# Layer 0 of a four-layer convolution net: the patch filter and the 3x3 taps folded into one map per channel

## The chip, the cores and the metric

The kernel runs on one core of one Trainium2 chip. A core has five engines with queues of their own: TensorE (PE in the profile; its weight loads are PEld), VectorE (DVE), ScalarE (ACT), GpSimd (POOL) and SyncE (SP), which here issues loads. 16 DMA engines move data between HBM and the on-chip memory SBUF; matrix products land in PSUM, which has 8 banks of 512 fp32 columns on 128 partitions. The metric is the device time of one execution in microseconds (us). All data is fp32.

## The reference

The input is x, 4 images of 64 channels of 256x256. Four layers follow each other, each of the form `x = x + layer(group_norm(x))`. Only layer 0 changes:

```python
def _gn(v, G=32, eps=1e-5):               # 32 groups of 2 channels, over the whole image
    ...
def _L0_conv_ref(x, w_in, w_dw, fft_filter, w_out):
    p = 8
    x = einsum('bchw,oc->bohw', x, w_in)             # 64 -> 384 channels
    xp = x.reshape(B, C, H//p, p, W//p, p).transpose(0, 1, 2, 4, 3, 5)
    xf = rfft2(xp) * fft_filter                      # one 8x5 filter per channel
    x = irfft2(xf) ... back to (B, C, H, W)          # within each 8x8 patch
    x = conv_general_dilated(x, w_dw, 3x3, padding 1, feature_group_count=C)
    x1, x2 = split(x, 2, axis=1)                     # 192 gates, 192 values
    x = gelu(x1) * x2
    return einsum('bchw,oc->bohw', x, w_out)         # 192 -> 64 channels
x = x + _L0_conv_ref(_gn(x), ...)
x = x + _L1_conv_ref(_gn(x), kernel)                 # dense 3x3, 64 -> 64
x = x + _L2_conv_ref(_gn(x), ...)                    # two 1x1 branches chosen by a mask
x = x + _L3_conv_ref(_gn(x), ...)                    # 2D FFT with 2 x 16x16 modes
```

The patch filter is linear and works inside an 8x8 patch; the 3x3 taps are linear too and reach one pixel into the neighbouring patches. Both act on each of the 384 channels alone.

## The kernel before

Layer 0 goes over 128 strips of 8 rows (32 for each image). For a strip it normalizes x on ACT (`normalize_x`, L256), transposes it on PE so that pixels lie on partitions (`transpose_x`, L396), takes each 8x8 patch to 64 real frequencies with a matrix (`transform_x`, L406), expands 64 to 384 channels (`expand`, L419) and multiplies by the filter while DVE moves the result out of PSUM (L422), and goes back to pixels with a matrix that also puts channels on partitions (`invert`, L457, moved out by ACT at L464). The 3x3 taps follow in two ways: for 256 of the 384 channels on PE, as nine products with 32x32 diagonal matrices (`depthwise`, L484: 16 of these side by side in the array), for the last 128 on DVE as eight multiply-adds over 2048 elements (`vector_tap`, L522). Then come GELU on ACT (L498, L530), the gate on DVE (L504, L537), the product with w_out (`project`, L550 and L559), the residual (L573), the sums for the next normalization (L581), and the store to x1 by POOL's queue (L590). Intermediate results stay in SBUF.

The order on PE, DVE, ACT and SP is written out by hand (`tc.manual_schedule`): the loop over t interleaves stages of strips t-1 to t+2. POOL's order is left to the tile framework. PSUM is four tiles of two banks, taken in turn by `pair`. Loads of x and of the residual are tied to chosen matmuls by `after`, so that they come spread over the strip. Sums for images 1 to 3 are taken on the way (`load_stats`, `next_stats`); those for image 0 come first of all.

Of the kernel before, what the change touches and what calls it, by code (L numbers as in the profile page):

```python
# [26 lines left out]
def _patch_dft():  # L27


    p = PATCH  # L30
    h, w = np.meshgrid(np.arange(p), np.arange(p), indexing="ij")
    rows, pick = [], []
    for kw in range(p // 2 + 1):
        edge = kw in (0, p // 2)
        for kh in range(p // 2 + 1 if edge else p):
            ang = 2 * np.pi * (kh * h + kw * w) / p
            sel = np.zeros((p, p // 2 + 1))
            sel[kh, kw] += 0.5 if edge else 1.0
            if edge:
                sel[(-kh) % p, kw] += 0.5  # L40
            rows.append(np.cos(ang).ravel())
            pick.append(sel.ravel())
            if not (edge and kh in (0, p // 2)):
                rows.append(np.sin(ang).ravel())
                pick.append(sel.ravel())
    fwd = np.array(rows)
    inv = np.linalg.inv(fwd)
    pick = np.array(pick)
    twice = lambda m: np.concatenate([m, m], 0)
    return twice(fwd.T), twice(inv.T), twice(pick).T  # L50
# [19 lines left out]
def _constants(H, W):  # L70
    f_blk, b_blk, pick = _patch_dft()
# [17 lines left out]
        "c_ident": np.eye(128), "c_avg32": avg32, "c_sel32": sel32, "c_fdft": f_blk, "c_bdft": b_blk, "c_pick": pick, "c_avg": avg, "c_avgp": avgp, "c_avgx": avgx,  # L89
# [5 lines left out]
def _layouts(i):  # L95


    order = np.r_[0:128, HID : HID + 128, 128:HID, HID + 128 : 2 * HID]
# [3 lines left out]
        "w_in": a["L0_conv_w_in"][order].T,  # L102
        "w_dw": a["L0_conv_w_dw"].reshape(2 * HID, 9)[order].reshape(3, 128, 9).transpose(1, 0, 2),
        "filt": a["L0_conv_fft_filter"].reshape(2 * HID, 40)[order].T,
        "w_out": a["L0_conv_w_out"].T,
# [13 lines left out]
class _Net:  # L119
    def __init__(self, ctx, tc, a):  # L120
# [15 lines left out]
        self.slots = ctx.enter_context(tc.tile_pool(name="slot", bufs=2))  # L136
# [138 lines left out]
    def _layer0(self, ctx, dst):  # L275
# [5 lines left out]
        def pair(name):  # L281

            return pp.tile([128, 2, 512], F32, tag=f"p{next(turn) % 4}", name=name)

        small = self.small = lambda name: pair(name)[:, 0, :]
        HW2 = W // 2
        NJ = H // 8
        NS = B * NJ
        Q = 32
        halves = [slice(0, C), slice(C, 128)]  # L290
        quarters = [slice(k * Q, (k + 1) * Q) for k in range(4)]

# [9 lines left out]
        with tc.tile_pool(name="l0a", bufs=1) as p_a:  # L302
            bst0 = new_bst0(0)

            flat = a["x"][0].rearrange("c (s h) w -> (c s) (h w)", s=2)
            avgs = [self.load(name, p_a) for name in ("c_avgp", "c_avgx")]
            for k in range(NJ):
                if k % 2 == 0:
                    two = self.slot(k // 2 % 3, f"st_{k}").rearrange("p r w -> p (r w)")
                t = two[:, 4 * W * (k % 2) : 4 * W * (k % 2 + 1)]  # L310
                nc.sync.dma_start(t, flat[:, 4 * W * k : 4 * W * (k + 1)])
                input_stats(t.rearrange("p (r w) -> p r w", w=W), k, bst0)
            self.group_norm(0, 0, bst0, avgs)

        cp = pool("l0c", 1)
        p_st, p_x, p_r, p_xn = pool("l0st", 2), pool("l0x", 2), pool("l0r", 2), pool("l0xn", 1)
        p_T, p_f, p_u, p_l = pool("l0xT", 1), pool("l0xf", 2), pool("l0up", 2), pool("l0l", 1)
        p_v, p_g, p_h = pool("l0v", 2), pool("l0g", 1), pool("l0h", 2)
        fdft, bdft = self.load("c_fdft", cp), self.load("c_bdft", cp)
        pick, filt = self.load("c_pick", cp), self.load("filt", cp)  # L320
        wdw = self.load("w_dw", cp)
        ps = small("psf")
        nc.tensor.matmul(ps[:, :384], pick, filt, start=True, stop=True)
        flt = cp.tile([128, 1, 384], F32, name="flt")
        nc.vector.tensor_copy(flt[:, 0, :], ps[:, :384])

        win = cp.tile([128, 384], F32, name="win")
        for s in range(2):
            nc.sync.dma_start(win[halves[s]], a["w_in"])

        wout = cp.tile([128, 4, C], F32, name="wout")
        for k in range(4):
            nc.sync.dma_start(wout[quarters[k]], a["w_out"][0:128].rearrange("(g q) o -> q g o", q=Q))
        woutc = cp.tile([128, C], F32, name="woutc")
        for s in range(2):
            nc.sync.dma_start(woutc[halves[s]], a["w_out"][128:HID])

        eye = cp.tile([128, Q], F32, name="eye")
        nc.vector.tensor_copy(eye, self.ident[:, 0:Q])
        for k in range(1, 4):  # L340
            nc.vector.tensor_add(eye, eye, self.ident[:, k * Q : (k + 1) * Q])
        diag = cp.tile([128, 2, 9, Q], F32, name="diag")
        for t in range(2):
            for k in range(9):
                nc.vector.tensor_scalar(diag[:, t, k, :], eye, wdw[:, t, k : k + 1], None, ALU.mult)

        place = lambda t: divmod(t, NJ)
        exists = lambda t: 0 <= t < NS
        x0, xns, xT, xf, ups, yt, lt, vt, ht, rt, po, bst1, gt = ({} for _ in range(13))

        def load_x(t, *sides, ins=None):
            b, j = place(t)
            if t not in x0:
                x0[t] = p_x.tile([128, 8, HW2], F32, tag="x", name=f"x0_{t}")
            for s in sides:
                d = nc.sync.dma_start(
                    x0[t][halves[s]], a["x"][b, :, 8 * j : 8 * j + 8, s * HW2 : (s + 1) * HW2]
                )
                if ins:
                    self.after(d, ins)  # L360


        def rows_of(t):
            b, j = place(t)
            if j > 0:
                return [(b, 8 * j - 2, 0, 4)]
            parts = [(b - 1, H - 2, 0, 1)] if t > 0 else []
            return parts + ([(b, 0, 1, 4)] if t < NS else [])

        def load_r(t, *sides, ins=None):  # L370
            if t not in rt:
                rt[t] = p_r.tile([128, 4, 2, HW2], F32, tag="r", name=f"r0_{t}")
            for b, row, lo, hi in rows_of(t):
                for s in sides:
                    d = nc.sync.dma_start(
                        rt[t][halves[s], lo:hi].rearrange("p k r w -> p (k r) w"),
                        a["x"][b, :, row : row + 2 * (hi - lo), s * HW2 : (s + 1) * HW2],
                    )
                    if ins:
                        self.after(d, ins)  # L380

        def normalize_x(t):
            if not exists(t):
                return

            xn = xns[t] = p_xn.tile([128, HW2 // 16, 2, 8, 8], F32, tag="xn", name=f"xn_{t}")
            self.normalize(
                xn.rearrange("p k n r w -> p r (k n) w"),
                x0.pop(t).rearrange("p r (m w) -> p r m w", w=8), 0, place(t)[0],
            )  # L390

        def transpose_x(t):
            xn = xns.pop(t)
            ps = pair(f"psT_{t}").rearrange("p z (k m) -> p (z k) m", m=128)
            for k in range(8):
                nc.tensor.transpose(ps[:, k, :], xn[:, k].rearrange("p n r w -> p (n r w)"), self.ident)  # L396
            xT[t] = p_T.tile([128, 8, 128], F32, tag="xT", name=f"xT_{t}")
            nc.scalar.copy(xT[t], ps)

        def transform_x(t):  # L400
            x = xT.pop(t)
            ps = pair(f"psF_{t}").rearrange("p n (k m) -> p n k m", m=C)
            for k in range(8):
                for n in range(2):
                    for s in range(2):
                        nc.tensor.matmul(  # L406
                            ps[halves[s], n, k], x[halves[n], k, halves[s]], fdft[halves[n]], start=True, stop=True
                        )
            xf[t] = p_f.tile([128, 2, 8, C], F32, tag="xf", name=f"xf_{t}")
            nc.scalar.copy(xf[t], ps)  # L410

        def expand(t, g, k):

            if k == 0:
                ups[t, g] = p_u.tile([128, 2, 4, 384], F32, tag="up", name=f"up_{t}_{g}")
            ps = pair(f"psu_{t}_{g}_{k}")
            for s in range(2):
                for n in range(2):
                    nc.tensor.matmul(  # L419
                        ps[halves[n], s, 0:384], xf[t][halves[s], n, 4 * g + k], win[halves[s]], start=True, stop=True  # L420
                    )
# [163 lines left out]
        def store(t, *sides, ins=None):  # L585
            if t not in rt:
                return
# [149 lines left out]

# [724 lines left out]
```

## Time and profile before

The kernel takes 7382.61 us (median of 3 runs, 7378.16 to 7394.91). The profiled execution has a span of 7394.8 us from its first instruction to its last; the page gives no other time for it, and the span is 12.2 us above the median.

| stretch (from the trace) | us | PE busy | DVE busy | ACT busy | DMA share | GB/s |
|---|---|---|---|---|---|---|
| start, sums of image 0 (0 to 90) | 90 | 27.22 | 57.66 | 14.21 | 0.61 | 216 |
| strips of layer 0 (90 to 4852) | 4762 | 4688.79 | 4384.48 | 2330.40 | 0.24 | 58 |
| layer 1 (4852 to 5532) | 680 | 669.71 | 607.83 | 486.54 | 0.91 | 220 |
| layer 2 (5532 to 6822) | 1290 | 1255.00 | 1117.73 | 1003.75 | 0.67 | 171 |
| layer 3 (6822 to 7395) | 573 | 507.53 | 268.79 | 93.66 | 0.93 | 358 |

The first matmul of layer 1 starts at 4851.89 us. In a group of instructions the profile gives the time in which at least one of them ran, and the mean of one: 16 small matmuls that run side by side count once in the first number. The DMA share is the mean busy share of the 16 DMA engines[...].

### The profile page before, as it was taken

The numbers are of one execution on the slowest core, as the hardware profiler recorded it, in microseconds if no ns is written. First come the engines' busy times: TensorE is split into PE (matmuls) and PEld (weight loads), VectorE is DVE, ScalarE is ACT, GpSimd is POOL, SyncE is SP. The second block draws the span as 40 slices with busy tenths as digits, with TensorE's granted clock in tenths as the row PEclk, the third lists the DMA queues.
The fourth block names the chain that finished last, engine by engine and source line by source line (L and its number), as shares of the span: only waits on it lengthen the run. The fifth ranks groups of instructions, "written<-read, shape, count | busy, mean of one in ns | idle before, by whom it ended". The sixth has DMA issues, their size and how long they took to land. (4 is left out here: it accounts for less than half of the span.)

```text
span 7394.8 us, 396673 instructions
## 1 busy us (share of the span) xinstructions
PE 7148.3 (97%) x188280; PEld 4274.7 (58%) x188280; DVE 6436.5 (87%) x5625; ACT 3928.6 (53%) x4181; POOL 659.3 (9%) x1435
## 2 busy tenths in 40 slices
PE   6999999999999999999999999999999999999998
PEld 4666666666666666666666666633334444444376
DVE  7999999999999999999999999889988888897445
ACT  3444444454454444444445545457778778776211
POOL 0000000000000000000000000011111222222011
PEclk9999999999999999999999999999999999999955
DMA  3222222222222222222111111279986676676989
GB/s 131 64 64 64 61 64 61 61 61 61 61 61 61 61 61 61 61 61 61 47 46 47 47 47 47 60 186 228 230 197 158 169 178 173 172 179 192 354 328 400
DMA packets 650136, 873.38 MB, mean 118 GB/s; under 512 B 43988, under 2 KB 470180, under 8 KB 646468
## 3 DMA queue, kind: packets, MB, share of 16 engines
q1 hardware_dynamic: 567492, 579.51, 29.4%
q0 software_dynamic: 81024, 268.50, 12.5%
q8 instruction: 1477, 24.20, 1.4%
q14 instruction: 143, 1.17, 0.1%
HBM read 579.41 MB, written 268.44 MB: 115 GB/s over the span
## 5 line engine op out<-in xcount | busy, mean ns | idle before, releaser
L484 PE MATMUL psd<-y,diag 32*32 32x512 f32 x73296 | 2535.6, 597 | 12.4 <-issue 10.7
L522 DVE SCALAR_TENSOR_TENSOR v<-y,sb_w_dw,v 128x2048 f32<-128x2048 f32 x1024 | 2391.5, 2335 | 112.1 <-ACT v L520 89.3
L484 PEld LDWEIGHTS psd<-y,diag 32*32 32x32 f32 x73296 | 1526.9, 103 | 858.8 <-issue 338.9
L464 ACT COPY y<-psy 128x512 f32<-128x512 f32 x1536 | 915.6, 660 | 1673.5 <-PE psy L457 1671.7
L422 DVE TENSOR_TENSOR up<-psu,flt 128x768 f32<-128x768 f32 x1024 | 933.1, 952 | 203.9 <-PE psu L419 203.2
L457 PEld LDWEIGHTS psy<-sb_c_bdft,up 64*64 64x64 f32 x49152 | 850.2, 135 | 343.3 <-issue 129.8
L457 PE MATMUL psy<-sb_c_bdft,up 64*64 64x64 f32 x49152 | 919.5, 221 | 25.0 <-issue 22.4
L419 PE MATMUL psu<-win,xf 64*64 64x384 f32 x8192 | 785.0, 488 | 20.9 <-DVE h L504 10.4
L1040 DVE TENSOR_TENSOR q<-xn 128x2313 f32<-128x2313 f32 (+2 forms) x256 | 627.8, 2494 | 1.7 <-ACT xn L256 1.7
L1095 PE MATMUL one<-z,wp 32*32 32x512 f32 x16384 | 594.1, 598 | 17.3 <-issue 13.4
L1041 ACT ACTIVATE q<-q 128x2313 f32<-128x2313 f32 (+2 forms) x256 | 528.9, 2086 | 31.4 <-DVE q L1040 29.9
L498 ACT ACTIVATE h<-psd 128x1024 f32<-128x1024 f32 x258 | 251.2, 1023 | 519.8 <-PE psd L484 519.7
L256 ACT ACTIVATE xn<-x,nb,r 128x1024 f32<-128x1024 f32 (+3 forms) x272 | 486.9, 1793 | 22.2 <-DMA x<-x 8.3
L1095 PEld LDWEIGHTS one<-z,wp 32*32 32x32 f32 x16384 | 368.4, 103 | 225.0 <-issue 82.7
L1054 PE MATMUL div<-q,ones 64*32 64x512 f32 x8192 | 466.2, 594 | 14.3 <-ACT q L1041 9.4
L429 POOL MEMSET y<- 128x22 f32 x384 | 52.2, 136 | 4264.3 <-ACT y L437 3209.8
L419 PEld LDWEIGHTS psu<-win,xf 64*64 64x64 f32 x8192 | 299.5, 134 | 192.1 <-issue 87.7
L1128 POOL DMA_DIRECT2D x<-r x512 | 273.6, 541 | 972.1 <-DVE r L1125 881.2
L854 PE MATMUL m<-t,wk 64*64 64x512 f32 x3072 | 341.1, 588 | 0.0
L1054 PEld LDWEIGHTS div<-q,ones 64*32 64x32 f32 x8192 | 151.8, 107 | 321.1 <-issue 253.6
L537 DVE TENSOR_TENSOR v<-g,v 64x1024 f32<-64x1024 f32 x257 | 313.2, 1219 | 9.3 <-ACT g L530 1.4
L504 DVE TENSOR_TENSOR h<-h,psd 128x1024 f32<-128x1024 f32 x258 | 302.7, 1215 | 7.5 <-PE psd L484 7.0
(156 smaller groups left out, 7400.4 us busy)
## 6 DMA issues: line engine op xcount, KB each, us to landing
x<-x SPq DMA_DIRECT2D x240, 640.0 KB, 6.3
x<-x SPq DMA_DIRECT2D x100, 1024.0 KB, 13.9
x<-in_x_dram SPq DMA_DIRECT2D x256, 256.0 KB, 3.8
x<-o POOLq DMA_DIRECT2D x128, 512.0 KB, 8.1
r<-x SPq DMA_DIRECT2D x512, 128.0 KB, 4.0
x<-r POOLq DMA_DIRECT2D x512, 128.0 KB, 4.0
r<-in_x_dram SPq DMA_DIRECT2D x248, 256.0 KB, 3.8
x<-r POOLq DMA_DIRECT2D x248, 256.0 KB, 3.3
```

The lines of the kernel that those rows point to most:

```text
L256: self.nc.scalar.activation(dst, src, AF.Identity, bias=self.nb[n][p0:p1, b : b + 1], scale=self.r[n][p0:p1, b : b + 1])
L419: nc.tensor.matmul(ps[halves[n], s, 0:384], xf[t][halves[s], n, 4 * g + k], win[halves[s]], start=True, stop=True)
L422: nc.vector.tensor_mul(ups[t, g][:, :, k, :], ps[:, :, 0:384], flt.broadcast_to([128, 2, 384]))
L457: nc.tensor.matmul(ps[halves[c], n, s, :, k, :], up[halves[n], s, k, i * 128 + c * C : i * 128 + (c + 1) * C], bdft[halves[n]], start=True ...
L464: nc.scalar.copy(yt[t][i][:, 3:11, w0 : w0 + 64].rearrange("p r (k n w) -> p n r k w", k=4, n=2), ps[:, :, s])
L484: ins = nc.tensor.matmul(d[q // 2][quarters[j], q % 2], diag[quarters[q], i, k, :], rows_in(t, i, quarters[q], j, dy)[:, :, dx : dx + W], ...
L522: nc.vector.scalar_tensor_tensor(v, s, wdw[:, 2, k : k + 1], v, ALU.mult, ALU.add)
L854: nc.tensor.matmul(rows2(m)[halves[j], s], w[dx][halves[s]], ts[n][halves[s], i, 2 * j : 2 * j + 2, dx : dx + W], start=(dx == 0), stop=(d ...
L1040: nc.vector.tensor_sub(d, p0, p1)
L1041: nc.scalar.activation(d, d, AF.Square)
L1054: ins = nc.tensor.matmul(ps[quarters[j], h], ones[halves[h]], q[n, g, k][halves[h], r + 2 * j : r + 2 * j + 2, o : o + W], start=(m == 0), ...
L1095: ins = nc.tensor.matmul(rows2(ps[g])[quarters[j], k], w[quarters[i]], z[quarters[i], h, 2 * j + dy : 2 * j + dy + 2, dx : dx + W], tile_p ...
```

## The change

The frequency route goes. The filter and the taps together are a linear map from a channel's patches to its output pixels, and that map depends on the channel alone. If the output cell is an 8x8 patch shifted by one pixel down and right, it needs 64 inputs of its "own" patch, and few of the right, lower and lower right neighbours. `tables` and `weights` build these maps on the chip at the start (128 channels at a time, copies on ACT and POOL) and write them to DRAM as `wts`.

The main loop works on 12 blocks (3 for each image), each of 11 cell rows: 11 x 34 = 374 columns. The 384 channels are taken in four parts of 96 (`kb`). For each part:

- `expand`: for each of 11 or 12 patch rows, 32 matmuls with the pixels as the stationary side and 96 columns of w_in as the moving side, so that pixels land on partitions; three copies (ACT and DVE by turns) put them into the one tile `u`, channel-major.
- `convolve`, 12 times: two gate and two value channels at once: 8 matmuls for the own patch (64x64, 374 columns) and 24 for the neighbours (16, 28 and 4 output rows); GELU on ACT, the gate on DVE, and a store of the result `h` to DRAM (`gs`) by POOL's queue. Its weights are loaded by `load_w`, one load for two convolves, three loads ahead.
- After `expand` and after the seventh convolve comes one `unit()`: the projection of one of 8 pixel rows of the block before. `load_g` reads its `g` back from DRAM with channels on partitions, `load_r` the residual; 32 matmuls, two adds, three sums, and a store.

PSUM becomes two tiles of four banks (`quad`). x for the next block is loaded and normalized between the convolves of the last part. After block 12 eight units remain by themselves. Layers 1 to 3 stay as they are; their SBUF slots are now taken after layer 0.

```diff
-        def pair(name):
-            return pp.tile([128, 2, 512], F32, tag=f"p{next(turn) % 4}", name=name)
+        def quad(name):
+            return pp.tile([128, 4, 512], F32, tag=f"p{next(turn) % 2}", name=name)
+        p_xn, p_x, p_st = pool("l0xn", NR + 1), pool("l0x", 2), pool("l0st", 2)
+        p_w, p_h = pool("l0w", 4), pool("l0h", 3)
...
+        def load_x(row, p_x=p_x):
+            b, i = row
+            x0[row] = p_x.tile([128, P, HW2], F32, tag="x", name=f"x0_{b}_{i}")
+            for s in range(2):
+                nc.sync.dma_start(x0[row][halves[s]], a["x"][b, :, P * i : P * i + P, s * HW2 : (s + 1) * HW2])
...
+        def expand(p, kb, t):
+            b, i0 = blocks[p]
+            ps = quad(f"psu_{p}_{kb}_{t}")
+            xn = xns[b, i0 + t]
+            for k in range(2):
+                for m in range(4):
+                    for s in range(2):
+                        for odd in range(2):
+                            nc.tensor.matmul(
+                                ps[halves[1 - odd], 2 * s + k, 2 * PB * m : 2 * PB * (m + 1)],
+                                xn[halves[s], 2 * (4 * k + m) + odd].rearrange("p r w -> p (r w)"),
+                                win[halves[s], kb, PB * (1 - odd) : PB * (3 - odd)], start=True, stop=True,
+                            )
...
+            nc.scalar.copy(at(slice(0, 128), 1), first)
+            lo, hi = halves
+            (nc.vector.tensor_copy if t % 2 else nc.scalar.copy)(at(hi, E2 + 1), second[lo])
+            nc.vector.tensor_copy(at(lo, O1), second[hi])
...
+        def convolve(p, kb, g):
+            ps = quad(f"pc_{p}_{kb}_{g}")
+            G = NG * kb + g
+            w = wl[p * (HID // 8) + G // 2]
...
+            for k in range(2):
+                for c in range(2):
+                    for h in range(2):
+                        nc.tensor.matmul(
+                            out(C * c, C, k, h), w[halves[h], k, 2 * (G % 2) + c, 0:C], cells(h, 4 * g + 2 * k + c, 0, 0),
+                            start=True, stop=False, tile_position=(h * C, c * C), skip_group_check=True,
+                        )
+            for n, (c0, m, down, right) in enumerate(UNITS):
...
+            nc.scalar.activation(h, v[:, 0], AF.Gelu)
+            nc.vector.tensor_mul(h, h, v[:, 1])
...
+            nc.gpsimd.dma_start(gs[p][:, 2 * G : 2 * G + 2].rearrange("k c p l -> (c p) k l"), h)
...
+        def load_g(p, r, half):
...
+                        nc.sync.dma_start(g1[halves[k], lo - q0 : hi - q0], gs[p][k, 0:C, at + lo : at + hi])
...
+        def load_unit(p, r):
...
+            load_r(p, r)
+            for half in range(2):
+                load_g(p, r, half)
...
+                for kb in range(4):
+                    for t in range(NR + 1):
+                        if 0 <= i0 + t < NP:
+                            expand(p, kb, t)
+                    unit()
+                    for g in range(NG):
+                        G = NG * kb + g
+                        if g % 2 == 0:
+                            load_w(p * (HID // 8) + G // 2 + 3)
+                        if kb == 3 and g < 2 and g < len(fresh):
+                            load_x(fresh[g])
+                        convolve(p, kb, g)
+                        self.next_norms()
+                        if g == NG // 2:
+                            unit()
+                        if kb < 3:
...
+                        else:
+                            for k in loaded[:1]:
+                                next_stats(b + 1, loaded.pop(0))
+                            if 0 <= g - 1 < len(fresh):
+                                k = g - 1
+                                normalize_x(fresh[k])
+                                if k + 2 < len(fresh):
+                                    load_x(fresh[k + 2])
```

The slices used above: `P` is 8, `PB` 48, `NG` 12, `NR` 11, `C` 64, `HID` 192; one packet of `h` in DRAM is a row of 374 fp32, 1496 bytes; one of the weights `w` is 1792 bytes; rows of x, residual and result are pieces of 128 fp32, 512 bytes.

## The prediction

> **What bounds the kernel now.** I read the slices first, then the stretches, then the groups of layer 0.
>
> Slices of the whole span (40 of 185 us):
>
> ```profile
> PE   6999999999999999999999999999999999999998
> PEclk9999999999999999999999999999999999999955
> DMA  3222222222222222222111111279986676676989
> ```
>
> PE is full from the second slice on; DMA idles for 26 slices, all of layer 0. The clock falls only at the end, in layer 3.
>
> Busy time by stretch (PE, PEld, DVE, ACT, POOL, then clock, DMA share, GB/s):
>
> ```profile
> 90.00:4852.00 4762.00, 4688.79 (x150103) 3091.40 (x150104) 4384.48 (x3604) 2330.40 (x2939) 245.66 (x679) 1.00 0.24 58
> 6822.00:7395.00 573.00, 507.53 (x3464) 334.12 (x3464) 268.79 (x474) 93.66 (x156) 53.52 (x74) 0.68 0.93 358
> ```
>
> In layer 0 PE (98%) ends nearly every wait and DVE (92%) is close behind; DMA has three quarters of its time free. The chain of waits reaches back only through layers 1 to 3, so here the stretch decides. Costliest groups:
>
> ```profile
> L484 PE MATMUL psd<-y,diag 32*32 32x512 f32 x73296 | 2535.6, 597 | 12.4 <-issue 10.7
> L522 DVE SCALAR_TENSOR_TENSOR v<-y,sb_w_dw,v 128x2048 f32<-128x2048 f32 x1024 | 2391.5, 2335 | 112.1 <-ACT v L520 89.3
> L464 ACT COPY y<-psy 128x512 f32<-128x512 f32 x1536 | 915.6, 660 | 1673.5 <-PE psy L457 1671.7
> L422 DVE TENSOR_TENSOR up<-psu,flt 128x768 f32<-128x768 f32 x1024 | 933.1, 952 | 203.9 <-PE psu L419 203.2
> L457 PE MATMUL psy<-sb_c_bdft,up 64*64 64x64 f32 x49152 | 919.5, 221 | 25.0 <-issue 22.4
> L498 ACT ACTIVATE h<-psd 128x1024 f32<-128x1024 f32 x258 | 251.2, 1023 | 519.8 <-PE psd L484 519.7
> L504 DVE TENSOR_TENSOR h<-h,psd 128x1024 f32<-128x1024 f32 x258 | 302.7, 1215 | 7.5 <-PE psd L484 7.0
> L854 PE MATMUL m<-t,wk 64*64 64x512 f32 x3072 | 341.1, 588 | 0.0
> L1054 PE MATMUL div<-q,ones 64*32 64x512 f32 x8192 | 466.2, 594 | 14.3 <-ACT q L1041 9.4
> ```
>
> The first number, divided by rounds of tiles that run together, is a round's price: m, four 64x64 tiles: 341.1/768 = 444 ns for 512 columns, 0.87 ns each; div, eight 64x32 tiles: 455 ns, 0.89; psy 75 ns for 64, 1.17; psd, 16 tiles: 553 ns.
>
> DMA prices, from stretches with one kind of packet (4 KB loads; 512-byte stores; 512-byte loads):
>
> ```profile
> 8.00:10.00 2.00, 0.00 (x0) 0.00 (x0) 1.99 (x5) 0.00 (x0) 0.00 (x0) 1.00 1.02 420
> 1501.00:1502.00 1.00, 1.00 (x29) 0.51 (x24) 0.95 (x2) 0.94 (x2) 0.00 (x0) 1.00 1.02 197
> 1508.00:1509.00 1.00, 1.00 (x55) 0.77 (x34) 0.97 (x2) 0.97 (x2) 0.00 (x0) 1.00 0.71 198
> ```
>
> Share x 16 engines / packets: 159 ns per 4 KB; 42.5 per 512-byte store; 29 per 512-byte load, though one starts only every 41 (387 a us). Between 29 and 159 a line gives 10.4 + 0.0363 per byte: 75.5 ns for 1792 bytes, 119 for 2992; for a store of 1496, with the stores' 13.5 on top, 78.
>
> **The Trainium skill.** *TensorEngine Tiling (Array Packing)*, PSUM Bottleneck, says that tiling speeds up TensorE but not the way out of PSUM; the 1673.5 us that ACT waits at L464 show the opposite balance so far. *TensorE: Matmul & The Clock Gate*, Part 1, says that the clock falls to half when PE was not busy enough in a window of some 3.4 us; here it is 1.00 in the strips and 0.68 in layer 3, where PE waits for DVE. *DMA: Bandwidth & Descriptors*, Issuing engines are not separate DMA queues, says that loads of SP and stores of POOL share the 16 engines. The trace of before never fills them in layer 0.
>
> **The change part by part.** All 4852 us up to layer 1 are replaced; the 2543 behind stay (first loads of layer 1 later by some 10 us, within the error).
>
> *PE.* For each part `kb` (48 in all): 11.33 expansions of 8 rounds of 96 columns, at 83 (0.87) to 112 ns (1.17), I take 100: 0.8 us. 12 convolves: two rounds of four, 2 x 325 ns, and three of eight, 3 x 333: 1.65 us. 2 projections: 4 rounds of four at 153, and 8 pairs of 128-row tiles, which no row shows, between 153 and 190 (0.87 to the 1.08 of psd): 2.0 us. Sum 33 us, 1580 over the layer against 4689.
>
> *Copies.* ACT at 0.71 ns an element from PSUM (660 at 512, 1023 at 1024): 842 for 768; DVE 952 (L422). Their targets lie 1640 bytes apart; L464, which scatters pieces of 32 bytes, is the nearest row. The program makes DVE's copy wait for ACT's of the same tile, so a tile is held for fill 0.8 + 0.84 + 0.84 + 0.95, or 0.8 + 0.84 + 2 x 0.95; with two tiles and some 0.1 for each hand-over a pair takes 3.8, 1.9 us each; DVE's own work is 1.43. GELU 0.83 and gate 0.93 for 748 elements: (1.65 + 0.83 + 0.93 + 0.35) / 2 = 1.9 per convolve.
>
> *DVE besides:* adds and sums of a unit 3.7 us, partly in the shade of PE; 4 us per kb uncovered. So one kb at full clock: 11.33 x 1.9 + 12 x 1.9 + 2 x 2.5 + 4 = 53 us.
>
> *Clock.* During expansions PE works 0.8 of 1.9 us. If that drops the clock, the fill doubles (pair 4.5: +4 us per kb) and the first convolves run at half for two windows (+3): 60. I take 60, the ends are 53 and 75 (half clock throughout: a convolve 3.3).
>
> *DMA, new.* h to DRAM and back and the weights, 572 MB that before did not move. Per kb, in time of all 16 engines: h 12 x 256 x 78 = 15.0 us; weights 6 x 256 x 75.5 = 7.2; g 2 x 768 x 119 = 11.4; residual 2 x 1408 x (29 to 41) = 5.1 to 7.2; result 2 x 1408 x 42.5 = 7.5; sums 3.4; together 50 to 52. The last kb of a block has no sums but all of x, 10.67 x 1024 x (29 to 41) = 20 to 28: 66 to 76. The cover is thus as long as what it covers, and bunched: between the projections before the first and after the seventh convolve (16 us of compute) fall one unit's loads, 8.8, and 12.5 of stores, 3.9 of weights and sums: 25.
>
> *Queues.* SP issues in order, some 0.5 us each (st 488 ns, r 622), and each load waits for the load eight before it. A unit is 16 loads, 8 us; behind them stand the weights needed six convolves (11 us) later, and in the last kb x, loaded only two convolves ahead of its normalization on ACT, behind which the next GELU stands. PE waits there. POOL's stores are queued behind the gate alone, and `h` has three buffers. I put +1 us on a plain kb, 61, and 85 on the last: 60 of compute against 71 of transfers, with x late twice.
>
> *Ends.* Start: before 90 us. Now DVE does 64 sums of 682 ns (44 us) and three tables of some 9, ACT 147 small copies of 0.3, POOL 36 DMAs with 1024 rows each, then 11 normalizations of 1.24 before the first copy out: 115. Tail: eight units alone, 11 us of loads that start only after the projection before, 3 of projection: 8 x 14 + 8 = 120.
>
> *Sum.* Block 3 x 61 + 85 = 268, x 12 = 3216; the first has no units and the last no next x, -75; + 235 = 3376. 7395 - 4852 + 3376 = **5919, I say 5920 us**. It stands against the span of 7394.8; the median is 12 lower, which changes nothing here.
>
> **The rivals.**
> - *Transfers hidden, clock kept.* A kb is 53, the last 58: 217 x 12 - 60 + 220 = 2764: 5307 us. For it: 25% DMA use today, 1.00 clock. Against: 50 us demand in 53, bunched.
> - *The queues become the bound.* Loads eight deep, packets of 1496 bytes at any address, contention as in layer 1 (share 0.91 at 220 GB/s): 80 for a kb, 110 for the last: 350 x 12 - 100 + 250 = 4350: 6893 us. For it: each late load stops SP, then PE, and PE's clock falls.
> - *Slower: the scattered copies.* No row shows single elements 1640 bytes apart. If a copy takes several times 842 and 952, three copies in a row hold the tile. From 268 to the 391 us a block that leaves no gain is 123, over 45.3 expansions 2.7 each: the copies would have to take about 2.5 times as long, over 2 us. At four times, 7 to 8 us an expansion, it ends near 8700. Against: L464 takes only 0.07 us more than the 593 ns that contiguous rows give (1023 less 512 at 0.84, the step between 64x512, 628, and 64x1024, 1057, at L530).
>
> That the work doesn't shrink on PE can't be: the matmuls are counted.
>
> **How the numbers follow.** 0.50 for the forecast (5600 to 6250), 0.24 for hidden transfers (5200 to 5600), 0.20 for the queues (6250 to 7100), 0.03 for slower, 0.03 elsewhere below. Leaving out a tenth at each side gives 5350 to 6500. Faster by over 0.2% (about what a measurement of this kernel can tell from no change) 0.965, within it 0.005, slower 0.03.
>
> **What would show it.** Right: expansions in pairs of 3.8 to 4.5 us with PE waiting for DVE; DMA share near 0.9 between 115 and 3300 us; PE's clock below 0.9 there; waits of PE for g or w after a unit, and of ACT for x in each fourth part; eight lone units of 14 us. Wrong, if a copy takes far from 0.84 or 0.95 us, if a 64x32 round of 374 columns is far from 333 ns, or if packets of 1496 bytes take well over 80 ns: then the term named is off and the sum with it.

## The result, and the profile after

The changed kernel takes 7474.0 us (median of four, 7463.13 to 7493.13) where the kernel before takes 7384.0 (7378.16 to 7394.91): the ratio is 1.0121, with a 95% interval from 1.0104 to 1.0138. It is 1.2% slower, and the forecast of 5920 us was wrong by 1550 us, in sign and in size.

The profiled execution of after has a span of 7461.4 us. The first expansion starts at 114.3 us, the last convolve ends at 4778.5, the tail of lone units at 4904.8, and the first product of layer 1 starts at 4918.1 (4851.9 before). The 2543 us behind it are what they were, so the whole difference, 66 us of span, lies in layer 0. Slices of the whole span of after:

```profile
PE   2777777778777777878787777689999999999997
PEclk8989989998898888889988999889999999999955
DMA  6456767676665766676756565799985766666989
```

Neither PE nor DMA is full between the second slice and the 26th. Busy time by stretch of after (columns as in the view before: PE, PEld, DVE, ACT, POOL, clock, DMA share, GB/s):

```profile
114.00:4905.00 4791.00, 3693.78 (x77848) 2052.54 (x77848) 2396.75 (x2108) 1907.73 (x1515) 584.46 (x787) 0.90 0.65 174
6888.00:7461.00 573.00, 506.03 (x3464) 333.20 (x3464) 266.27 (x471) 93.58 (x156) 52.31 (x72) 0.68 0.93 356
```

PE's work in layer 0 shrank by 995 us, from 4688.79 to 3693.78, where the forecast had 1580 left. DVE's fell from 4384 to 2397. DMA stands at 0.65, not near 0.9. So the work did shrink, but PE now waits a quarter of the time. The costliest groups of layer 0 on the page of after:

```profile
L443 PE MATMUL psu<-win,xn 64*64 64x96 f32 x34816 | 1080.4, 287 | 887.4 <-DVE u L455 685.4
L502 ACT ACTIVATE h<-pc 128x748 f32<-128x748 f32 x576 | 456.4, 792 | 1829.8 <-PE pc L495 1700.1
L503 DVE TENSOR_TENSOR h<-h,pc 128x748 f32<-128x748 f32 x576 | 536.3, 931 | 1248.3 <-ACT h L502 1248.1
L495 PE MATMUL pc<-u,w 64*16 64x374 f32 (+2 forms) x27648 | 1249.0, 485 | 0.1
L452 ACT COPY u<-psu 128x768 f32<-128x768 f32 x544 | 871.4, 1607 | 632.8 <-PE psu L443 629.8
L455 DVE COPY u<-psu 64x768 f32<-64x768 f32 x544 | 871.2, 1606 | 365.0 <-ACT u L454 347.4
L486 PE MATMUL pc<-u,w 64*64 64x374 f32 x9216 | 894.8, 497 | 88.1 <-DVE h L503 72.4
```

Two things are to be seen. First, the counts: a convolve issues 8 own and 24 neighbour matmuls, and there are 576 of them, so 4608 and 13824; the page has 9216 and 27648. Every matmul of the program stands in the records twice. Secondly, GELU (792 ns) and gate (931) are as forecast, but the copies of 768 elements into `u` take 1607 ns on ACT and on DVE alike, where the forecast had 842 and 952.

Some expansions of after in order of time (start, duration, engine, in brackets the idle time before and what ended it):

```profile
2064.00 1.55 PE L443 MATMUL psu<-win,xn 64*64 64x96 f32 x64 [0.89 <-DVE u L455]
2064.89 1.60 DVE L454 COPY u<-psu 64x768 f32<-64x768 f32 x1 [0.94 <-ACT u L452]
2065.68 1.60 ACT L452 COPY u<-psu 128x768 f32<-128x768 f32 x1 [0.82 <-PE psu L443]
2066.50 1.60 DVE L455 COPY u<-psu 64x768 f32<-64x768 f32 x1
2067.30 1.61 ACT L454 COPY u<-psu 64x768 f32<-64x768 f32 x1
2068.24 1.55 PE L443 MATMUL psu<-win,xn 64*64 64x96 f32 x64 [2.69 <-DVE u L455]
2068.94 1.62 DVE L455 COPY u<-psu 64x768 f32<-64x768 f32 x1 [0.84 <-ACT u L454]
2070.61 1.55 PE L443 MATMUL psu<-win,xn 64*64 64x96 f32 x64 [0.82 <-DVE u L455]
```

Two expansions start at 2064.00 and 2068.24, and the third, which begins the next pair, at 2070.61: 6.6 us for a pair (forecast 3.8 to 4.5). PE fills a tile in 1.55 us, not 0.8, and then waits for three copies in a row of 1.6 us. Waits of after between 1000 and 3000 us (engine, line, what it waited for, us in total, times, longest):

```profile
ACT h L502 <- PE pc L495: 713.5, 194, 10.7
PE psu L443 <- DVE u L455: 278.9, 146, 3.8
ACT xn L258 <- DMA x<-in_x_dram: 122.0, 38, 11.3
ACT h L502 <- DMA g<-h: 74.7, 21, 6.4
```

In the convolves the readers wait for PE; in the expansions PE waits for the copies. Waits for transfers are the small ones. Split by phase in the trace (means over the ten blocks between the first and the last, from matmul to matmul), in us per `kb`:

| | forecast | after, kb 0 to 2 | after, kb 3 |
|---|---|---|---|
| expansions | 21.5, and up to 7 for the clock | 42.6 | 41.2 |
| 12 convolves | 22.8 | 42.0 | 52.4 |
| two projections on PE | 5 | 11.2 | 11.5 |
| whole part | 61 | 95.8 | 105.0 |

A block is 392 us. The forecast had said that 391 leave no gain.

### The profile page after: what moved, and what is told of

It is laid out like the page before. It is cut to its first block, busy times and chain, and to the rows that moved or that the text cites. A ratio compares the mean times of both kernels' runs of the same rounds, so it can differ in the third digit from the quotient of the medians.

```text
span 7461.4 us, 251651 instructions
## 1 busy us (share of the span) xinstructions
PE 6129.1 (82%) x115416; PEld 3223.4 (43%) x115416; DVE 4470.5 (60%) x4164; ACT 3536.2 (47%) x2900; POOL 1052.0 (14%) x1646
## 4 chain that ended last, share of the span: by engine, by line
PE 60%; DMA 12%; ACT 10%; DVE 8%; issue 8%; SPq 2%; POOL 1%; ACTq 0%; DVEq 0%; POOLq 0%
PE pc L495 10%; PE m L850 9%; PE psu L443 7%; PE one L1091 7%; PE pc L486 7%; PE div L1050 6%; ACT u L452 5%; DVE u L455 5%; DMA x<-in_x_dram 4%; PE po L584 4%; ACT u L454 3%; DMA st<-in_x_dram 3%; PE psz L1080 2%; PE po L591 2%; DMA g<-g 2%
## 5 line engine op out<-in xcount | busy, mean ns | idle before, releaser
L443 PE MATMUL psu<-win,xn 64*64 64x96 f32 x34816 | 1080.4, 287 | 887.4 <-DVE u L455 685.4
L443 PEld LDWEIGHTS psu<-win,xn 64*64 64x64 f32 x34816 | 974.0, 164 | 1014.4 <-ACT u L452 280.8
L502 ACT ACTIVATE h<-pc 128x748 f32<-128x748 f32 x576 | 456.4, 792 | 1829.8 <-PE pc L495 1700.1
L503 DVE TENSOR_TENSOR h<-h,pc 128x748 f32<-128x748 f32 x576 | 536.3, 931 | 1248.3 <-ACT h L502 1248.1
L495 PE MATMUL pc<-u,w 64*16 64x374 f32 (+2 forms) x27648 | 1249.0, 485 | 0.1
L452 ACT COPY u<-psu 128x768 f32<-128x768 f32 x544 | 871.4, 1607 | 632.8 <-PE psu L443 629.8
L455 DVE COPY u<-psu 64x768 f32<-64x768 f32 x544 | 871.2, 1606 | 365.0 <-ACT u L454 347.4
L486 PE MATMUL pc<-u,w 64*64 64x374 f32 x9216 | 894.8, 497 | 88.1 <-DVE h L503 72.4
L258 ACT ACTIVATE xn<-x,nb,r 128x1024 f32<-128x1024 f32 (+3 forms) x272 | 486.5, 1792 | 459.2 <-DMA x<-in_x_dram 313.2
L506 POOL DMA_DIRECT2D g<-h x576 | 417.1, 724 | 1842.5 <-DVE h L503 1732.2
L454 DVE COPY u<-psu 64x768 f32<-64x768 f32 x272 | 437.3, 1608 | 339.8 <-ACT u L452 336.9
L1050 PE MATMUL div<-q,ones 64*32 64x512 f32 x8192 | 465.5, 595 | 12.6 <-ACT q L1037 9.2
L454 ACT COPY u<-psu 64x768 f32<-64x768 f32 x272 | 437.9, 1610 | 6.6
```

The source lines that it names most:

```text
L443: nc.tensor.matmul(ps[halves[1 - odd], 2 * s + k, 2 * PB * m : 2 * PB * (m + 1)], xn[halves[s], 2 * (4 * k + m) + odd].rearrange("p r w -> ...
L452: nc.scalar.copy(at(slice(0, 128), 1), first)
L454: (nc.vector.tensor_copy if t % 2 else nc.scalar.copy)(at(hi, E2 + 1), second[lo])
L455: nc.vector.tensor_copy(at(lo, O1), second[hi])
L486: nc.tensor.matmul(out(C * c, C, k, h), w[halves[h], k, 2 * (G % 2) + c, 0:C], cells(h, 4 * g + 2 * k + c, 0, 0), start=True, stop=False, ...
L495: nc.tensor.matmul(out(q, m, k, h), w[halves[h], k, 2 * (G % 2) + c, c0 : c0 + m], cells(h, 4 * g + 2 * k + c, down, right), start=False, ...
```

## The experiments

My theory after the result: each matmul costs TensorE twice what I took (I had divided by the records and not by the matmuls), and the copies pay for writing single elements; the two add up. Rivals: the transfers and queues of the forecast hold the stage; or the low clock does. Where no interval is given, a kernel was timed once, and the weight lies on its trace. The runs were spread over several chips, on which the kernel before took 7384 to 7446 us, so differences between single timings are good to some 60 us, and the split by phase counts for more. Times of expansions are means over all four parts of a block and those of twelve convolves means over parts 0 to 2, unless a part is named.

**Writes of the copies: the order turned.** In `expand`, the copies walk channel, group, cell instead of group, cell, channel:

```diff
-            v = ps[:, :, 0 : 8 * PB].rearrange("p s (m c) -> p s m c", m=4)
+            v = ps[:, :, 0 : 8 * PB].rearrange("p s (m c) -> p c s m", m=4)
-            at = lambda h, o: u[h, :, t * CW + o : t * CW + o + n].rearrange("p c (s m) -> p s m c", s=4)
+            at = lambda h, o: u[h, :, t * CW + o : t * CW + o + n].rearrange("p c (s m) -> p c s m", s=4)
-            first, second = v[:, :, :, 0:PB], v[:, :, :, PB : 2 * PB]
+            first, second = v[:, 0:PB], v[:, PB : 2 * PB]
```

> The layout of u is kept; only the order in which the copies walk is turned: channel outermost, so that writes come in runs of 16 elements and reads of PSUM step by 384 bytes. If only scattered writes cost (theory of the write side): copies at 842 and 952 ns, about 6650 us, convolves unchanged at 3.53. If reading PSUM in single elements costs as much as writing in single elements: copies stay near 1600 ns and the time near 7470. Transfers theory: above 7300 whatever the copies take.

It takes 6840.1 us, 0.9255 of before (0.9240 to 0.9271). Groups of this run between 1000 and 3000 us:

```profile
L452 ACT COPY u<-psu 128x768 f32<-128x768 f32 x264 | 224.2, 849 | 337.1 <-PE psu L443 336.7
L454 DVE COPY u<-psu 64x768 f32<-64x768 f32 x132 | 125.7, 952 | 133.0 <-ACT u L452 132.4
L454 ACT COPY u<-psu 64x768 f32<-64x768 f32 x132 | 105.6, 800 | 3.2
L455 DVE COPY u<-psu 64x768 f32<-64x768 f32 x264 | 253.3, 960 | 127.9 <-ACT u L454 125.7
```

The same elements, read and written in another order, take 800 to 849 ns on ACT and 952 to 960 on DVE: what the forecast had. The expansions of a part fall from 42.2 to 29.6 us (25 was expected; they keep waits for the gate and for the copies' chain), the convolves stay at 42.0, and so the time is 6840 and not 6650. The scattered order cost 634 us, of which 12.6 us over 48 parts, some 605, are in the expansions. Reading PSUM in steps of 384 bytes costs the copies little or nothing (the next run shows by how little). The clock rose as the waits went, from 0.93 to 0.97 between 1000 and 2000 us and from 0.88 to 0.96 between 2000 and 3000. The rival of the clock as a cause of its own was not tried apart from this.

**Writes of the copies: another layout.** `u` with the channel innermost, so that TensorE reads in steps of 192 bytes:

```diff
-u = pool("l0u", 1).tile([128, PB, (NR + 1) * CW + 2], F32, name="u")
+u = pool("l0u", 1).tile([128, (NR + 1) * CW + 2, PB], F32, name="u")
...
-tensor=v.tensor, offset=v.offset + down * CW + o, ap=[v.ap[0], [CW, NR], [step, 2], [1, HC]]
+tensor=v.tensor, offset=v.offset + PB * (down * CW + o), ap=[v.ap[0], [PB * CW, NR], [PB * step, 2], [PB, HC]]
```

> One map per channel kept, but u stored with the channel innermost, so that the copies out of PSUM write runs of 48 channels (192 bytes) and not single elements 1640 bytes apart; TensorE in turn reads its moving columns 192 bytes apart. Scattered-copies theory: the copies fall from 1607 ns to about 842 (ACT) and 952 (DVE), a pair of expansions from 6.6 us to about 1.55 + 0.84 + 0.84 + 0.95 + 0.3 = 4.5, the expansions of one kb from 42 to about 25 us, 48 x 17 = 820 us in all: about 6650 us, if a convolve stays at 3.53 us. If TensorE pays for the wide steps, as it may, the convolves grow and eat the gain. Transfers theory: DMA work is the same, so no more than 150 us are gained: above 7300. If the clock is what matters, it should rise from 0.90 towards 0.95 or more in this stage.

It takes 8659.6 us, 1.1715 of before (1.1697 to 1.1732). The copies are at full speed here too, and the expansions take 25.6 us a part; but twelve convolves take 85.7 us in place of 42, the case that the expectation had named without a price. Groups by shape between 1000 and 3000 us, first of this run, then of after:

```profile
L486 PE MATMUL pc<-u,w 64*64 64x374 f32 x3144 | 565.0, 833 | 9.6 <-DVE h L503 9.6
L452 ACT COPY u<-psu 128x768 f32<-128x768 f32 x180 | 143.7, 798 | 177.9 <-PE psu L443 177.9
```

```profile
L486 PE MATMUL pc<-u,w 64*64 64x374 f32 x3904 | 375.6, 495 | 36.6 <-DVE h L503 36.6
```

Busy time by record: 565.0/3144 against 375.6/3904, 1.87 times. TensorE pays for the wide steps as the copies do, so the layout of the changed kernel is the better of the two, and it is the order of writing that had to change. ACT's copies, which here read and write runs of 48, take 798 ns (L452) and 791 (L454, by the same view); with PSUM read in steps they took 849 and 800. For L454 the steps thus cost no more than 9 ns; the 51 of L452 come up again in the next run. PE is 93% busy here at clock 1.00 and the DMA share is 0.53: PE's work alone can fill this stage.

**Run length.** As the turned copies, but walking group, channel, cell, so that four elements (16 bytes) are written in a row:

```diff
-            v = ps[:, :, 0 : 8 * PB].rearrange("p s (m c) -> p s m c", m=4)
+            v = ps[:, :, 0 : 8 * PB].rearrange("p s (m c) -> p s c m", m=4)
-            ...rearrange("p c (s m) -> p s m c", s=4)
+            ...rearrange("p c (s m) -> p s c m", s=4)
```

> As the run with turned copies, but with writes in runs of four elements (16 bytes), then a step of 1640 bytes, where that run had runs of 16. If the penalty is paid once per step to a new place: four times as few steps, a copy takes about (1607 - 842) / 4 more than 842, some 1030 ns on ACT and 1120 on DVE, and the time is about 7000. If a run of four is long enough to hide it: 849 and 960 ns and 6840. If only long runs help: near 1600 ns and 7470.

It takes 6915.4 us. Groups between 1000 and 3000 us:

```profile
L455 DVE COPY u<-psu 64x768 f32<-64x768 f32 x261 | 261.2, 1001 | 134.7 <-ACT u L454 132.6
L452 ACT COPY u<-psu 128x768 f32<-128x768 f32 x261 | 260.9, 1000 | 306.3 <-PE psu L443 305.9
L454 DVE COPY u<-psu 64x768 f32<-64x768 f32 x131 | 124.7, 952 | 132.6 <-ACT u L452 132.0
L454 ACT COPY u<-psu 64x768 f32<-64x768 f32 x130 | 108.2, 832 | 3.1
```

Neither expectation holds as a whole: ACT's L452 is near the penalty by step (1000, 1030 expected), L454 pays little or nothing on either engine. The Trainium skill, *SBUF — State Buffer*, Specifications (TRN2), says that SBUF has lines of 16 bytes and wants at least two hits in each. By the offsets, if `u` itself starts on a line, the runs of L452 and L455 start 4 or 12 bytes into a line, so that one element falls alone on its line; those of L454 start at 0 or 8. Against the 798 ns of runs of 48, L452 on ACT pays 202 ns for 192 lone elements here, 51 for 48 in the turned copies and 809 for 768 in after: 1.05 to 1.06 ns for each. In these three there are as many runs as lone elements, so a price by the run would fit them as well. But L454 here has as many runs with none alone and pays 41 ns (832 against 791). And the run with planes, below, happens to move the starts: there 24 elements of each copy are alone, with 48 runs as in the turned copies, and L452 falls from 849 to 826 while L454 rises from 800 to 818. So on ACT the account fits better than any by runs; the 41 ns it leaves open. On DVE it does not: L455 takes 959 in the other layout, 960 with 48 alone, 1001 with 192, and then 1606 with 768. That stays open, and no run was made to shift the addresses alone.

**TensorE's price: the neighbours twice.** The cleanest place to measure it is the convolve of after, where PE is the bound:

```diff
-            for n, (c0, m, down, right) in enumerate(UNITS):
+            for n, (c0, m, down, right) in enumerate(UNITS + UNITS):
...
-                                start=False, stop=(n == 2), ...
+                                start=False, stop=(n == 5), ...
```

> The kernel of the change with the 24 neighbour matmuls of each convolve issued twice, so that the neighbours' part is counted twice in h; nothing else differs. It measures the disputed cost by itself: if three rounds of eight 64x32 tiles on 374 columns cost 2.1 us, a convolve goes from 3.53 to 5.65 us and the time up by 576 x 2.1 = 1220 us: about 8690. With the 1.0 us of my forecast the sum of TensorE's work would be 2.65 us, hidden or nearly so behind copies and transfers: 7474 to 8050. If transfers set the time: up by less than 300.

It takes 8420.2 us, on a chip where the kernel before took 7446. The group of the neighbours on the page of this run, to be held against the 1249.0 us in after:

```profile
L495 PE MATMUL pc<-u,w 64*16 64x374 f32 (+2 forms) x55296 | 2353.9, 480 | 0.6 <-issue 0.4
```

The 1104.9 us more are 1.92 us for the 24 matmuls of a convolve, 0.64 a round, 1.71 ns a column against the 0.89 of the forecast; and twelve convolves take 65.0 us in place of 42.0. The time is above what the forecast's prices (at most 8050) and the transfers (less than 300 more) allow. The transfers are the same and the DMA share falls to 0.56 to 0.59. The expected 1220 us are 946 for three reasons that the split shows: 1.92 us and not 2.1; the fourth part grows by 14 us instead of 21, as its late x is now covered; and the expansions are 2 us shorter.

**The neighbours left out.**

```diff
-            for n, (c0, m, down, right) in enumerate(UNITS):
+            for n, (c0, m, down, right) in enumerate(()):
...
```

> Leaves out part of the computation: the 24 matmuls of each convolve for the three neighbouring patches, so only the own patch goes into h. Theory of the doubled TensorE price: a convolve falls from 3.53 us to the chain (1.45 + 0.83 + 0.93 + 0.35) / 2 = 1.8, that is 576 x 1.75 = 1000 us less: about 6460. With the prices of my forecast (a round of 374 columns 0.33 us) the three rounds cost 1.0 us and, with the chain at (0.65 + 0.83 + 0.93 + 0.35) / 2 = 1.4 against 1.9, the gain is 290 us: about 7180. Transfers theory: little gain, since DMA work is the same: about 7300 to 7470, with the DMA share near 0.9.

It takes 7406.5 us: neither of the two numbers for TensorE, but within the 7300 to 7470 of the transfers theory. That theory's sign, a DMA share near 0.9, is not there: it is 0.67 and 0.69. A stretch of this run (columns as above), and waits between 1000 and 3000 us:

```profile
1000.00:2000.00 1000.00, 573.84 (x10592) 379.69 (x10588) 517.63 (x469) 394.64 (x314) 124.48 (x168) 0.82 0.67 180
```

```profile
ACT h L502 <- PE pc L486: 383.2, 124, 8.8
ACT h L502 <- DMA g<-h: 321.1, 85, 8.4
```

Now the GELU waits for the stores of `h` (74.7 us in after). There are three buffers, and each is held for GELU 0.79, gate 0.93 and the store, which in these 2000 us takes 8.0 from the start of POOL's issue to the landing (median): 9.7 us, so by this sum 3.2 us a convolve. Twelve convolves take 37.6 us, 3.1 each. PE waits more, the clock falls to 0.82 and 0.81 and the expansions grow to 45.3. So there was a bound just below TensorE's 3.5 us that I had not priced: the time for which a store holds its buffer, with a third of the DMA engines' time free. The run could not tell the PE price; the next ones take this bound away.

**Without the traffic of h.** First the stores and loads alone, then with the neighbours left out as well:

```diff
-            nc.gpsimd.dma_start(gs[p][:, 2 * G : 2 * G + 2].rearrange("k c p l -> (c p) k l"), h)
-            g1 = p_1.tile([128, 4, L], F32, tag="g1", name=f"g1_{p}_{r}_{half}")
-            ...
+            loads[p, r, half] = fixed[0]
```

> Leaves out the stores of h to DRAM and the loads of it (the projections work on a fixed tile instead), 26 of some 52 us of DMA work per kb, with the 768-row loads and most of the entries in the queues of SP and POOL. Transfers and queues theory: a large gain, 500 us or more: below 7000. Doubled TensorE price and scattered copies: only the late loads of the fourth part and of the tail go, 11 x 10 + 8 x 4 = 140 us at most: 7330 to 7470.

> Leaves out the 24 matmuls for the neighbouring patches in each convolve and the stores and loads of h (projections work on a fixed tile), to be set against the run that leaves out the stores and loads of h alone (7239 us): without stores no buffer of h can be late. Doubled TensorE price: a convolve falls from 3.53 to 1.8 us, 576 x 1.73 = 1000 us less: about 6250, up to 6500 if a lower clock makes the expansions longer. With the prices of my forecast: 576 x 0.5 = 290 less, about 6950.

The first takes 7239.0 us, 235 less than after: more than the 140 expected and less than half of the transfers theory's 500. The tail gives 71 (56 us, from 126), the fourth part 9 a block (105.0 to 95.8), and the other parts 1.5 to 3, at a clock of 0.94 to 0.96. With the neighbours left out as well it takes 6585.6, 653 less. Twelve convolves take 26.5 us, 2.2 each; 42 to 26.5 over 48 parts are 744 us, and part of it comes back in the fourth part, 88.3 us against 78.8 for the rest, where x is late again. The doubled price had said 1000 less, mine 290. The expansions are hardly longer (40.5 against 40.1); what is missing from the 1000 is that a convolve takes 2.2 us in the mean, not 1.8, and late x. The chain itself was priced right: away from the projections the GELUs of the trace start 1.3 and 2.1 us apart by turns, 1.7 in the mean. The two intervals behind each projection take 2.5 to 3.1: there DVE first has the adds and sums of the unit to do, and the gate stands behind them.

**What is left in the turned version.** First the two halves of `u` in separate planes, so that the copies of a tile write separate ranges; then, on top, four x buffers in one pool with those of the sums and earlier loads, four h buffers, three of weights, and the sum of the residual with the column outermost (the addresses in `expand` and `cells`, which follow the planes, and the moved loads are left out here):

```diff
-tile([128, PB, (NR + 1) * CW + 2], F32, name="u")
+tile([128, 2, PB, UL], F32, name="u")
...
```

```diff
-p_xn, p_x, p_st = pool("l0xn", NR + 1), pool("l0x", 2), pool("l0st", 2)
-p_w, p_h = pool("l0w", 4), pool("l0h", 3)
+p_xn, p_x = pool("l0xn", NR + 1), pool("l0x", 4)
+p_w, p_h = pool("l0w", 3), pool("l0h", 4)
...
-            v = rv[:, 1:7].rearrange("p (b k) n -> p b k n", k=2)
-            nc.vector.tensor_add(v, v, pv[:, 0:3])
+            v = rv[:, 1:7].rearrange("p (b k) n -> p n b k", k=2)
+            nc.vector.tensor_add(v, v, pv[:, 0:3].rearrange("p b k n -> p n b k"))
```

> The turned copies of the run before, and u split into two planes (even and odd cells), so that the copies of one tile write separate ranges and DVE's no longer waits for ACT's. If the chain of copies holds the tile: a pair of expansions is then two fills of 1.55 us with 0.2 of hand-over, 3.4 us in place of 5, the expansions of one kb go from 29.6 to about 20 us, 48 x 9.6 = 460 us less: about 6380. If transfers now set the time (63 us of all 16 engines per kb, by the DMA share of 0.78 over kbs of 82 us), part of it comes back as waits for g, x and free h buffers: 6500 to 6800.

> On top of the two planes: four x buffers shared with the sums (x of the next block loaded from the end of the third part on), four h buffers in place of three (three of weights in place of four), and the sum of the residual walked with the column outermost, six writes in a row. If late x and occupied h buffers are what is left: 8 us in each fourth part, 88 in all, about 2 us per kb for h, 96, and 0.85 us in the shade of each of 96 sums, up to 80: 150 to 260 below the run with two planes, about 6150 to 6200. If the transfers' throughput is the bound, less than 60 below it.

The planes bring nothing: 6839.5 us, 0.9241 (0.9226 to 0.9257), and DVE still waits for ACT's copy of the same tile. Groups of this run, in which L453 and L455 are the L452 and L454 of before:

```profile
L453 ACT COPY u<-psu 128x768 f32<-128x768 f32 x270 | 223.0, 826 | 342.8 <-PE psu L444 342.6
L455 DVE COPY u<-psu 64x768 f32<-64x768 f32 x135 | 128.5, 952 | 138.4 <-ACT u L453 138.0
L455 ACT COPY u<-psu 64x768 f32<-64x768 f32 x135 | 110.5, 818 | 3.3
```

So it is not the overlap of the ranges in `u` that ties them; but both planes still lie in one tile `u`, and the run does not clear the tile as such. It may also be the PSUM tile, of which both read the same banks: the Trainium skill, *PSUM — Partial Sum Buffer*, PSUM bank collisions raise a hardware error, says that two engines must not use one bank and quadrant (32 partitions) at once. That would cover DVE's first copy behind ACT's L453, which reads all partitions, but not DVE's last copy, L456, behind ACT's L455: these read different halves of the partitions. What ties the copies stays open; copies with banks of their own were not tried.

The second takes 6769.6 us, 0.9141 of before (0.9123 to 0.9159), and is the fastest version here. It gains 70 us, not 150 to 260: the fourth part falls from 92.3 to 88.4 us only, as its expansions grow by 4 (why, was not followed), and the other parts by 0.9. What each of the changes gave was not tried apart. ACT no longer waits for x or for buffers of `h`: both waits are gone from these 2000 us. The sum of the residual did what it should; the first line is from the run with planes, the second from this one, by shape, between 1000 and 3000 us:

```profile
L601 DVE TENSOR_TENSOR r<-r,po 128x1056 f32<-128x1056 f32 x30 | 63.8, 2126 | 101.2 <-PE po L594 83.3 <-DMA r<-in_x_dram 13.3 <-DMA g<-g 4.6
```

```profile
L601 DVE TENSOR_TENSOR r<-r,po 128x1056 f32<-128x1056 f32 x32 | 40.2, 1255 | 118.4 <-PE po L594 113.8 <-DMA g<-g 4.6
```

These 0.87 us seem to lie in the shade of PE, for which DVE waits just before. Last, the same without the traffic of h:

> The best kernel so far (6770 us) without the stores and loads of h (the projections work on a fixed tile). If TensorE and the copies set the time there too: only the tail (60 us) and some 2 to 4 us per kb go, 6520 to 6640. If transfers are its bound (65 us of all engines per kb): the expansions and convolves leave 72 to 75 us per kb against 83, and it falls to 6300 or less.

It takes 6577.3 us, on the chip where before took 7446 (7405 for the run it is held against), within what TensorE and the copies predict. Parts 0 to 2 take 79 us against 82, so in the fastest version the transfers of `h` cost 3 us a part and most of the tail (50 us without them, 126 with). Stretches of this run (columns as above):

```profile
1000.00:2000.00 1000.00, 880.70 (x19868) 461.39 (x19860) 469.95 (x560) 328.08 (x391) 42.50 (x57) 0.99 0.47 106
2000.00:3000.00 1000.00, 886.65 (x20040) 467.21 (x20040) 472.21 (x558) 331.19 (x394) 43.52 (x58) 0.98 0.48 109
```

PE is 88% busy with half of the DMA time free. What is left between PE's 88% and all of it is mainly the wait for DVE's copies in the expansions, 151.5 of 233 idle us between 1000 and 3000.

## Why the prediction was wrong, point by point

- *PE*, the step that failed most. I took busy time over rounds of records. The line `x73296` for L484 and `x3072` for one of three groups of L854 could have told: the program of before has 36936 matmuls at L484 and 3072 at L854, the trace 73872 and 6144 when all groups of these lines are added. A round of 512 columns in m costs 341.1/384 = 888 ns, not 444, and all prices of the step double. Measured: fill 1.55 us (0.8 forecast), convolve 3.5 (1.65), projection 5.6 (2.0). The first two are double; what else is in the projection was not taken apart. PE's sum, 33 us a part in the forecast, is 72 in the turned version (85% of 85.1). The Trainium skill, *FP8 and Floating Point Precision*, TensorE Precision Notes, says that true FP32 takes 4 passes through the array; the trace shows two records a matmul and 1.73 ns a column, and no run here counts the passes. With TensorE as measured and the forecast's copies, a part would be near 25 + 42 + 11 = 78 us; the run with turned copies has 83 (93 for the fourth).
- *Copies*. 1607 ns instead of 842 and 952. I had named the risk, taken L464 with its pieces of 32 bytes for the nearest row, and given it 0.03. A piece of eight elements does not show what single elements cost: this was the second step that failed, and the sign of the result hangs on it. Undoing it gives back 634 us.
- *The rival "slower"* said that copies would have to take about 2.5 times as long, over 2 us. By its own chain it is more: 2.7 us more an expansion are 5.4 a pair, so the three copies of a tile would have to take 8 us in place of 2.63, three times; and at four times an expansion would take 6 us, not 7 to 8. They took 1.6 each, which by itself would not have sufficed; with fills of 1.55 in place of 0.8 the pair came to 6.6 us and a block to 392. The rivals were priced one at a time on a base that was itself wrong, and the two errors had the same sign. That the time came out so near to that of before is chance.
- *GELU and gate*: 0.79 and 0.93, as forecast. That a convolve is set by (fill + GELU + gate) / 2 did not hold: PE alone is longer, and below it lie the three h buffers at 3.1 us (3.2 by their sum), which the step *Queues* mentioned and did not price.
- *Clock*: it fell, to 0.88 to 0.93 (0.90 over the layer), as said. It lengthens a record of the fill from 252 ns (in the last run) to 292; I estimate from this 0.21 us a fill of 1.55, 2.4 us a part, where I had put 7.
- *DMA* and *Queues*: the share is 0.65, over 98 us a part 64 us of all engines against 56 on average in the forecast. It was 14% more, but beside 98 us of compute most of it hides: without the traffic of `h` 235 us are gained. Between 1000 and 3000 us of after, packets took longer than priced: 172 ns for the 2992 bytes of `g` (119 forecast), 102 for the 1792 of the weights (75.5), 41 for 512-byte loads (29 to 41). Not so the stores of `h`: most of their packets hold three rows, 4488 bytes and not the 1496 that were assumed, and take 209 ns, 70 a row (78). That the trace of before never fills the engines in layer 0 is contradicted by the forecast's own line at 1501 us, share 1.02; it holds for longer stretches (0.24 over the layer). The fourth part is longer by 9.2 us and not 24, with late x in it (ACT waits 122 us for x between 1000 and 3000).
- *Ends*: start 114.3 (115), tail 126 (120), the layers behind 2543 (2543): right.

Sum of it: from 6840 to 7474 by the scattered writes, which a run shows; from 5920 to 6840 by TensorE's price and what hangs on it, which is what is left over and was not measured as one step.

## What to carry to other kernels

Before a duration from a profile becomes a price, hold its count against the loops of the code: here a count of the matmuls in the old kernel's loops would have shown two records for each and cut the expected gain by more than half: the turned version, whose copies take what was forecast, gains some 550 us and not 1475. When a copy changes layout, count the elements it writes in a row, not its total: here the fast order was the one that writes runs and lets PSUM be read in steps. And an experiment that removes a bound shows the next one, as the three h buffers did; price the buffers of each stage before calling it hidden.

## What was not expected of the hardware

- Writing single fp32 elements 1640 bytes apart takes 2.09 ns each on ACT and on DVE (1607 for 768), runs of 16 take at most 849 and 960. Four in a row are nearly enough (832 to 1001), six in a row too (1255 for 1056, from 2126 for single ones 32 bytes apart).
- On ACT the loss fits the number of elements that stand alone on a line of 16 bytes by their address: 1.05 to 1.06 ns for each of 48, 192 and 768 of them at L452, where 24 alone in as many runs as 48 take 826 ns and not 849. On DVE it does not fit (960 with 48 alone, 1001 with 192, 1606 with 768).
- Reading PSUM in steps of 384 bytes hardly slows the copies: 800 ns on ACT and 952 on DVE (L454), where runs of 48 on both sides take 791 and 951.
- TensorE's moving operand in steps of 192 bytes costs 1.87 times as much as runs of 17 elements (four 64x64 tiles, 374 columns).
